# A convolution and state-space kernel: another order of the work, a convolution with stationary weights, and replicated loads in two halves on two DMA queues

## The chip, the cores and the metric

The program runs on one core of a Trainium2 chip. The core has five engines that run side by side, each with its own instruction stream: TensorE (PE in the profile; its weight loads stand apart as PEld), VectorE (DVE), ScalarE (ACT), GpSimd (POOL) and SyncE (SP). They share a memory of 128 partitions (SBUF) and a small one for sums (PSUM), and wait for each other through semaphores. Transfers between SBUF and the chip's main memory (DRAM) run on 16 DMA engines; an instruction on SP or ACT issues one, and each of the two has its own DMA queue.

The metric is device time in microseconds of one execution. The time before is the median of three runs.

## The reference

Four layers are computed on an input of shape (2, 128, 128, 128): batch, channels, rows, columns, all in float32. Layers 0 and 2 are the same function with different weights, and they hold what is changed. Cut to that:

```python
y = conv3x3(x, conv_w) + conv_b                  # 128 -> 128 channels
seq = y.reshape(B * H * W, 8, 16)                # a row of a channel: 8 tokens of 16 features
xz = einsum('nld,ed->nle', seq, in_proj_w)
xi, z = split(xz, 2)                             # 32 and 32
xc = silu(causal_conv1d(xi, conv1d_w) + conv1d_b)
dt, Bm, Cm = split(einsum('nld,ed->nle', xc, x_proj_w), [1, 17])
dt = softplus(dt * dt_proj_w + dt_proj_b)        # 8 tokens x 32
dA = exp(dt[..., None] * A)                      # 32 x 16 states, A = -exp(A_log)
dBx = dt[..., None] * Bm[:, :, None, :] * xc[..., None]
# over the 8 tokens:
h = dA[t] * h + dBx[t]
ys[t] = sum_n(h * Cm[t])
ym = (ys + D * xc) * silu(z)
out = ym @ out_proj_w.T                          # back to 16 features
# group norm over 4 groups of channels, silu, and x is added
```

Layer 1 is a gate from the density of 8 x 8 windows, and layer 3 a block of two convolutions with batch norm over the whole batch. The change does not touch these.

## The kernel before

One batch at a time goes through layer 0 (`_mamba`, `_group_norm`), layer 1 (`_density_gate`) and layer 2 (`_mamba`, `_group_norm`); layer 3 (`_basic_block`) follows for both. So `_mamba` runs four times.

In `_mamba` the image is cut into 32 tiles of four rows. One row of one channel, 128 numbers, is one sequence of 8 tokens x 16 features, so a tile has 4 x 128 = 512 sequences, and they lie along the free dimension. The state of one token, 32 inner channels x 16 states for each sequence, is 512 rows of 512 sequences, held as `NJ` = 4 blocks on 128 partitions. Within a block the partition is (n, e): 16 states n, each with `DJ` = 8 channels e.

The stages of a tile are small functions:

- `conv` (L274) runs one image row per call: for each of nine taps the 128 pixels of the row are the stationary operand and the tap's weights the moving one, 128 columns each, 36 matmuls a tile. The result has the row's columns on the partitions, so the tokens and their features, as `project` needs them. VectorE adds the bias (L293).
- `project` (L301) makes xc and z, each by two matmuls and a silu on ScalarE.
- `steps` (L315) makes dt by softplus, u = dt * xc on GpSimd (L324), and stores u into DRAM as `su` with two DMAs (L327).
- `inout` (L332) makes B and C, stores both into DRAM as `sb` (L344) and multiplies them (`prod`, L346). C of a token is stored with B of the same token.
- `own` (L348) makes the part of the output that a token gives to itself.
- `load` (L358) reads, for token t, eight rows of `su` back into all 16 groups of partitions (`ur`, 1024 KB, L363), and 16 rows of `sb` into eight partitions each (`bcr`, 512 KB, L368). These are the replicated loads. Both are issued on SP.
- `inject` (L370) multiplies `ur` and B on GpSimd into `h`.
- `token` (L375) does for each half of the blocks: two matmuls into `set` (L391), the exponential (L399), and on VectorE the product with the old state (L401), the product with C (`r`, L402) and the sum into the new state (L406). Then four matmuls sum `r` over the states into `ys` (L409). After tokens 3 and 7, VectorE adds `t1` (L420) and GpSimd multiplies by silu(z) (L421). After token 7, `finish` (L426) multiplies by the output weights, copies, takes statistics and stores.

The order is set in two steps. `put` (L445) lists each call under a step; there are `STEPS` = 7 steps a tile, one for each of the tokens 1 to 7, and a tile's earlier stages stand under negative steps, beside the tokens of the tile before. The calls are traced in that order, and the framework's scheduler then orders each engine's instructions by priority and by when it expects their inputs and buffers. Each engine executes its own stream in order. Buffers limit how far one can run ahead: three of `ur`, five of `bcr`, four of `h`, two of `r`, two of `set`, two of the common PSUM tile `one`.

Of the kernel before, what the change touches and what calls it, by code (L numbers as in the profile page):

```python
# [31 lines left out]
P = 128  # L32
NT, FT = 8, 16
DI, DS, DC = 32, 16, 4
NQ = 4
NJ = DI * DS // P
DJ = DI // NJ
NG = 4
# [11 lines left out]
def _constants(H):  # L50

    parts = {}


    neg = np.zeros((NJ, NQ, DJ, NQ, DS, DJ), np.float32)
    red = np.zeros((DS, DJ, NQ, NQ, DJ), np.float32)
    gsum = np.zeros((2, NQ, DS, 2, NJ, NQ, DJ), np.float32)
    for q in range(NQ):
        for e in range(DJ):
            neg[:, q, e, q, :, e] = -1.0  # L60
            red[:, e, q, q, e] = 1.0
        for g in range(2):
            gsum[g, q, :, g, :, q, :] = 1.0
    parts["neg"] = neg.reshape(P, -1)
    parts["red"] = red.reshape(P, -1)
    parts["gsum"] = gsum.reshape(P, -1)
    parts["group"] = np.kron(np.eye(NG), np.full((CG, CG), 1.0 / CG)).astype(np.float32)
    parts["ident"] = np.eye(P, dtype=np.float32)
    parts["neghalf"] = np.full((P, CG), -0.5, np.float32)
    for name, n in (("wy", H), ("wx", P)):  # L70
        _, frac = _bilinear(n)
        parts[name] = np.tile(frac[None, :], (P, 1))
    return _packed(parts)
# [24 lines left out]
def _mamba_layout(w):  # L98
# [24 lines left out]
    alog = np.zeros((NJ, NQ, DJ, NQ, DS, DJ), f32)  # L123
    po = np.zeros((P, NT, DI), f32)
    by_d = wx.reshape(-1, NJ, DJ)
    for q in range(NQ):
        pdt1[:, q, :, :, q, :] = by_d[0][:, :, None, None]
        pdt2[:, q, :, :, q, :] = w["dt_proj_w"][:, 0].reshape(NJ, DJ)[None, None, :, :]
        pb[:, q, :, q, :] = by_d[1 : 1 + DS].transpose(1, 2, 0)
        pc[:, q, :, q, :] = by_d[1 + DS :].transpose(1, 2, 0)  # L130
        for e in range(DJ):
            alog[:, q, e, q, :, e] = w["A_log"].reshape(NJ, DJ, DS)[:, e, :]
    for t in range(NT):
# [10 lines left out]
            "conv_b": np.tile(w["conv_b"][None, :], (P, 1)),  # L144
# [104 lines left out]
STEPS = NT - 1  # L249
AT_CONV, AT_XC, AT_DT, AT_BC, AT_G = -11, -7, -6, -6, -4  # L250
AHEAD_LOAD, AHEAD_B = 4, 2


def _mamba(tc, src, w, con, dst, scratch, stats, H):
# [14 lines left out]
    live = {}  # L269

# [3 lines left out]
    def conv(k, part):  # L274

        if part == 0:
            if k % (BAND // ROWS) == 0:
                live["band"] = _load_band(nc, bandp, src, k * ROWS, BAND, H)
            live[k] = {"py": one(), "band": live["band"]}
        xb, py = live[k]["band"], live[k]["py"]  # L280
        r = part
        for tap in range(9):
            kh, kw = divmod(tap, 3)
            nc.tensor.matmul(  # L284
                py[:, r * P : (r + 1) * P],
                lhsT=xb[:, (k * ROWS) % BAND + r + kh, kw : kw + P],
                rhs=w["conv"][:, tap, :],
                start=(tap == 0),
                stop=(tap == 8),
            )  # L290
        if part == ROWS - 1:
            y = seq.tile([P, NS], F32, tag="y", name="y")
            nc.vector.tensor_tensor(  # L293
                y.rearrange("p (r c) -> p r c", r=ROWS),
                py.rearrange("p (r c) -> p r c", r=ROWS),
                w["conv_b"].unsqueeze(1).to_broadcast([P, ROWS, P]),
                ALU.add,
            )
            live[k]["y"] = y

    def project(k):  # L301
# [3 lines left out]
        zs = s["zs"] = seq.tile([P, 2, NS], F32, tag="zs", name="zs")  # L305
# [9 lines left out]
    def steps(k):  # L315

        s = live[k]
        dt = s["dt"] = seq.tile([P, 2, NS], F32, tag="dt", name="dt")
        for g in range(2):
            pd = one()  # L320
            nc.tensor.matmul(pd, lhsT=w["dt"], rhs=s["xc"][:, g, :], start=True, stop=True)  # L321
            nc.scalar.activation(dt[:, g, :], pd, AF.Softplus, bias=w["dt_b"])  # L322
        u = s["u"] = seq.tile([P, 2, NS], F32, tag="u", name="u")
        nc.gpsimd.tensor_tensor(u, dt, s["xc"], ALU.mult)  # L324
        su = s["su"] = scratch.tile([NT, DJ, NJ, NS], F32, tag="su", name="su")
        for g in range(2):
            nc.sync.dma_start(  # L327
                out=su[g * NQ : (g + 1) * NQ].rearrange("q e j s -> j (q e) s"),
                in_=u[:, g, :],
            )  # L330

    def inout(k):  # L332

        s = live[k]
        bc = tmp.tile([P, 2, NS], F32, tag="bc", name="bc")
# [7 lines left out]
        sb = s["sb"] = scratch.tile([NT, DS, 2, NS], F32, tag="sb", name="sb")  # L343
        nc.sync.dma_start(out=sb.rearrange("t n i s -> (t n) i s"), in_=bc)  # L344
        prod = s["prod"] = tmp.tile([P, NS], F32, tag="prod", name="prod")
        nc.gpsimd.tensor_tensor(prod, bc[:, 0, :], bc[:, 1, :], ALU.mult)  # L346

    def own(k):  # L348

        s = live[k]  # L350
        t1 = s["t1"] = seq.tile([P, 2, NS], F32, tag="t1", name="t1")
        for g in range(2):
            p = one()
            nc.tensor.matmul(p, lhsT=gsum[:, g, :], rhs=s["prod"], start=True, stop=True)  # L354
            nc.scalar.copy(t1[:, g, :], p)  # L355
        nc.gpsimd.tensor_tensor(t1, t1, s["u"], ALU.mult)  # L356

    def load(k, t):  # L358

        s = live[k]  # L360
        if t < NT - 1:
            ur = s["ur", t] = st.tile([P, NJ, NS], F32, tag="ur", name="ur", bufs=3)
            nc.sync.dma_start(  # L363
                out=ur,
                in_=s["su"][t].unsqueeze(0).to_broadcast([DS, DJ, NJ, NS]),
            )
        bcr = s["bcr", t] = st.tile([P, 2, NS], F32, tag="bcr", name="bcr", bufs=5)
        nc.sync.dma_start(out=bcr, in_=s["sb"][t].unsqueeze(1).to_broadcast([DS, DJ, 2, NS]))  # L368

    def inject(k, t):  # L370
        s = live[k]
        b = s["h", t] = st.tile([P, NJ, NS], F32, tag="h", name="h", bufs=4)
        nc.gpsimd.tensor_tensor(b, s["ur", t], s["bcr", t][:, 0:1, :].to_broadcast([P, NJ, NS]), ALU.mult)  # L373

    def token(k, t):  # L375
# [3 lines left out]
        if t == 1:  # L379
            s["ys"] = [None, None]  # L380
        if t == 1 or t == NQ:
            s["ys"][g] = ps_y.tile([P, NS], F32, tag=f"ys{g}", name="ys")
            nc.tensor.matmul(s["ys"][g], lhsT=w["d"], rhs=s["xc"][:, g, :], start=True, stop=False)
        ys = s["ys"][g]
        r = st.tile([P, NJ, NS], F32, tag="r", name="r", bufs=2)
        for jp in range(2):
            pt = ps_set.tile([P, 2, NS], F32, tag="set", name="set")
            for i in range(2):
                j = 2 * jp + i
                a = j * NQ * DJ  # L390
                nc.tensor.matmul(  # L391
                    pt[:, i, :],
                    lhsT=w["rep"][a : a + NQ * DJ, q, :],
                    rhs=s["dt"][a : a + NQ * DJ, g, :],
                    start=True,
                    stop=True,
                    tile_position=(a, 0),
                )
            nc.scalar.activation(pt, pt, AF.Exp)  # L399
            js = slice(2 * jp, 2 * jp + 2)  # L400
            nc.vector.tensor_tensor(pt, pt, s["h", t - 1][:, js, :], ALU.mult)  # L401
            nc.vector.tensor_tensor(  # L402
                r[:, js, :], pt, s["bcr", t][:, 1:2, :].to_broadcast([P, 2, NS]), ALU.mult
            )
            if t < NT - 1:
                nc.vector.tensor_tensor(s["h", t][:, js, :], pt, s["h", t][:, js, :], ALU.add)  # L406
        for j in range(NJ):
            a = j * NQ * DJ
            nc.tensor.matmul(  # L409
                ys[a : a + NQ * DJ, :],  # L410
# [6 lines left out]
        if q == NQ - 1:  # L417

            v = seq.tile([P, NS], F32, tag=f"v{g}", name="v")
            nc.vector.tensor_tensor(v, ys, s["t1"][:, g, :], ALU.add)  # L420
            nc.gpsimd.tensor_tensor(v, v, s["zs"][:, g, :], ALU.mult)  # L421
            s["v", g] = v
        if t == NT - 1:
            finish(k)

    def finish(k):  # L426
        s = live.pop(k)
        po = one()
        for r in range(ROWS):
            for g in range(2):  # L430
                nc.tensor.matmul(  # L431
                    po[:, r * P : (r + 1) * P],
# [5 lines left out]
        o = seq.tile([P, NS], F32, tag="o", name="o")  # L438
        nc.scalar.copy(o, po)
        nc.vector.bn_stats(stats[:, k, :], po)  # L440
        nc.sync.dma_start(out=dst[:, k * ROWS : (k + 1) * ROWS, :].rearrange("p r w -> p (r w)"), in_=o)
# [3 lines left out]
    def put(k, at, f, *args):  # L445
        todo.setdefault(k * STEPS + at, []).append((f, (k, *args)))

    for k in range(ntile):
        for t in range(1, NT):
            put(k, t - 1, token, t)  # L450
        for part in range(ROWS):
            put(k, AT_CONV + part, conv, part)
        put(k, AT_XC, project)
        put(k, AT_DT, steps)
        put(k, AT_BC, inout)
        put(k, AT_G, own)
        for t in range(NT):
            put(k, t - AHEAD_LOAD - 1, load, t)
            if t < NT - 1:
                put(k, t - AHEAD_B - 1, inject, t)  # L460
    for at in sorted(todo):
        for f, args in todo[at]:
            f(*args)
# [309 lines left out]
```

## Time and profile before

| what | value |
|---|---|
| median of three runs | 10826.29 us (10817.6 to 10827.49) |
| profiled execution, its own time | 10815.53 us |
| its span, first to last instruction | 10813.7 us |
| granted clock of TensorE, mean | 0.897 |
| DMA moved | 1855.67 MB, mean 172 GB/s |

The page cuts the span into 40 slices of 270 us. The four runs of `_mamba` are the long stretches with DMA near 8 tenths; the gaps between are group norm and the gate, and the last 1.1 ms are layer 3. An engine's busy time does not count the time in which it waits in place or issues DMAs. A line of waits reads: who waited, for whom, the total in us, how often, the longest. A line of the chain reads: start, length, what ran.

### The profile page before, as it was taken

How to read it: one execution, taken by the hardware profiler on the slowest of the kernel's cores; microseconds unless marked ns; L12 is line 12 of the kernel's file. 1: busy time of each engine (PE TensorE's matmuls, PEld its weight loads, DVE VectorE, ACT ScalarE, POOL GpSimd, SP SyncE). 2: the span in 40 equal slices, each digit the busy share in tenths (PEclk: the TensorE clock that was granted, in tenths of full speed). 3: DMA queues.
4: the chain of work that ended last, by engine and by line, in shares of the span. 5: the costliest groups of instructions: out<-in, count | busy, mean ns of one | idle time of the engine just before them, and what ended most of it. 6: DMA issues, size and time to landing. Idle time of an engine off the chain costs nothing. (4 is left out here: it accounts for less than half of the span.)

```text
span 10813.7 us, 97333 instructions
## 1 busy us (share of the span) xinstructions
PE 8964.8 (83%) x36376; PEld 3550.2 (33%) x36376; DVE 6885.4 (64%) x6330; ACT 4590.3 (42%) x4841; POOL 5187.4 (48%) x1810
## 2 busy tenths in 40 slices
PE   7888888865888888858888888865888888859995
PEld 3333333243333333313333333253333333314442
DVE  5777777725777777756777777725777777740102
ACT  4555555422555545434555555312555555520112
POOL 5565656502666656526566566402665566620000
PEclk9999999856999999979999999756999999979997
DMA  8888888714888888868888888615888888861003
GB/s 200 202 198 198 201 199 203 176 66 116 200 203 200 196 196 203 191 193 207 199 201 201 199 200 204 170 45 133 197 202 202 199 197 199 199 182 44 22 0 118
DMA packets 510325, 1855.67 MB, mean 172 GB/s; under 512 B 42240, under 2 KB 163616, under 8 KB 395168
## 3 DMA queue, kind: packets, MB, share of 16 engines
q1 hardware_dynamic: 500640, 1815.90, 70.4%
q10 hardware_dynamic: 9216, 33.56, 0.8%
q8 instruction: 289, 4.73, 0.2%
q14 instruction: 180, 1.47, 0.1%
HBM read 1631.19 MB, written 218.10 MB: 171 GB/s over the span
## 5 line engine op out<-in xcount | busy, mean ns | idle before, releaser
L373 POOL TENSOR_TENSOR h<-ur,bcr 128x2048 f32<-128x2048 f32 x896 | 4052.8, 4526 | 2826.1 <-DMA bcr<-sb 1403.4
L399 ACT ACTIVATE set<-set 128x1024 f32<-128x1024 f32 x1792 | 1805.6, 1008 | 3009.5 <-PE set L391 2989.0
L401 DVE TENSOR_TENSOR set<-set,h 128x1024 f32<-128x1024 f32 x1792 | 2198.8, 1228 | 1007.7 <-ACT set L399 873.8
L409 PE MATMUL ys<-r,ct 128*32 128x512 f32 x7168 | 2021.5, 647 | 248.0 <-DVE r L402 247.8
L402 DVE TENSOR_TENSOR r<-set,bcr 128x1024 f32<-128x1024 f32 x1792 | 2189.0, 1222 | 48.5
L391 PE MATMUL set<-dt,rep 32*128 32x512 f32 x7168 | 2060.8, 653 | 5.0 <-DVE h L406 4.9
L406 DVE TENSOR_TENSOR h<-set,h 128x1024 f32<-128x1024 f32 x1536 | 1865.1, 1214 | 6.1 <-POOL h L373 6.1
L284 PE MATMUL one<-conv,band 128*128 128x128 f32 x9216 | 1415.1, 292 | 235.6 <-POOL band L169 215.7
L284 PEld LDWEIGHTS one<-conv,band 128*128 128x128 f32 x9216 | 1152.7, 193 | 1366.4 <-issue 1034.7
L391 PEld LDWEIGHTS set<-dt,rep 32*128 32x128 f32 x7168 | 545.0, 186 | 1077.1 <-issue 623.9
L399 ACT ACT_TABLE_LOAD x612 | 785.2, 1283 | 10.8
L354 PE MATMUL one<-prod,ct 128*128 128x512 f32 x512 | 412.9, 953 | 422.9 <-POOL prod L346 422.9
L409 PEld LDWEIGHTS ys<-r,ct 128*32 128x32 f32 x7168 | 266.8, 111 | 1300.6 <-DVE r L402 885.0
L641 DVE BATCH_NORM_STATS2 st<-pc 128x6 f32<-128x512 f32 x128 | 89.5, 699 | 904.2 <-ACT Y L640 904.2
L420 DVE TENSOR_TENSOR v<-ys,t 128x512 f32<-128x512 f32 x256 | 177.0, 691 | 759.4 <-PE ys L409 757.5
L633 PE MATMUL pc<-band,w 128*128 128x512 f32 x1152 | 496.1, 593 | 87.7 <-DVE w L625 87.7
L339 PE MATMUL one<-xc,keep 128*64 128x512 f32 x1024 | 535.3, 619 | 36.5 <-ACT dt L322 36.1
L431 PE MATMUL one<-keep,v 128*128 128x128 f32 x2048 | 348.5, 325 | 243.5 <-POOL v L421 243.5
L356 POOL TENSOR_TENSOR t<-t,u 128x1024 f32<-128x1024 f32 x128 | 299.8, 2343 | 500.1 <-ACT t L355 500.1
L633 PE MATMUL pc<-hband,w 128*128 128x512 f32 x1152 | 497.5, 595 | 6.3 <-ACT hband L675 6.3
L167 POOL MEMSET band<- 128x20 f32 x96 | 11.5, 125 | 906.2 <-PE pc L633 513.1
L640 ACT COPY Y<-pc 128x512 f32<-128x512 f32 x128 | 74.9, 585 | 874.3 <-PE pc L633 874.3
(110 smaller groups left out, 6841.8 us busy)
## 6 DMA issues: line engine op xcount, KB each, us to landing
ur<-su SPq DMA_DIRECT2D x896, 1024.0 KB
bcr<-sb SPq DMA_DIRECT2D x1024, 512.0 KB
su<-u SPq DMA_DIRECT2D x256, 256.0 KB
sb<-bc SPq DMA_DIRECT2D x128, 512.0 KB
band<-x SPq DMA_DIRECT2D x56, 640.0 KB
y<-o SPq DMA_DIRECT2D x128, 256.0 KB
g<-y SPq DMA_DIRECT2D x64, 512.0 KB
xr<-x SPq DMA_DIRECT2D x64, 512.0 KB
```

The lines of the kernel that those rows point to most:

```text
L284: nc.tensor.matmul(py[:, r * P : (r + 1) * P], lhsT=xb[:, (k * ROWS) % BAND + r + kh, kw : kw + P], rhs=w["conv"][:, tap, :], start=(tap = ...
L339: nc.tensor.matmul(p[g * NQ * DS : (g + 1) * NQ * DS, :], lhsT=w[m], rhs=s["xc"][:, g, :], start=True, stop=True)
L354: nc.tensor.matmul(p, lhsT=gsum[:, g, :], rhs=s["prod"], start=True, stop=True)
L373: nc.gpsimd.tensor_tensor(b, s["ur", t], s["bcr", t][:, 0:1, :].to_broadcast([P, NJ, NS]), ALU.mult)
L391: nc.tensor.matmul(pt[:, i, :], lhsT=w["rep"][a : a + NQ * DJ, q, :], rhs=s["dt"][a : a + NQ * DJ, g, :], start=True, stop=True, tile_posi ...
L399: nc.scalar.activation(pt, pt, AF.Exp)
L401: nc.vector.tensor_tensor(pt, pt, s["h", t - 1][:, js, :], ALU.mult)
L402: nc.vector.tensor_tensor(r[:, js, :], pt, s["bcr", t][:, 1:2, :].to_broadcast([P, 2, NS]), ALU.mult)
L406: nc.vector.tensor_tensor(s["h", t][:, js, :], pt, s["h", t][:, js, :], ALU.add)
L409: nc.tensor.matmul(ys[a : a + NQ * DJ, :], lhsT=red[:, q, :], rhs=r[:, j, :], start=False, stop=(q == NQ - 1), tile_position=(0, a),)
L431: nc.tensor.matmul(po[:, r * P : (r + 1) * P], lhsT=s["v", g][:, r * P : (r + 1) * P], rhs=w["out"][:, g, :], start=(g == 0), stop=(g == 1),)
L633: nc.tensor.matmul(pc, lhsT=w[:, tap, :], rhs=xb[:, rr + kh : rr + kh + ROWS, kw : kw + P], start=(tap == 0), stop=(tap == 8),)
```

## The change

It has six parts, all in `_mamba` and its weights.

1. The convolution is turned round: nine matmuls of 512 columns a tile with the weights stationary, spread in six calls over the slots -22 to -16, with the channels on the partitions, bias by ScalarE, and then four transposes on TensorE (`turn`) with a copy on ScalarE.
2. A step becomes two slots (`SLOTS` = 14 a tile), one for each half of a token. The sums into `ys` are a call of their own (`gather`), two slots after their half tokens; so are `gate`, `out` (in two halves), `product`, `scaled` and `own_u`.
3. The instructions of TensorE, ScalarE, VectorE and GpSimd keep the order in which they are written (`manual_schedule`); SP's queue is not in that list.
4. Partitions of the state are ordered (half of the channels, n, channel within the half) instead of (n, e). The constants and weights follow.
5. `load` is called twice for each token, once for each half of the partitions: the lower half on SP, the upper on ScalarE's queue one slot later.
6. `sb` holds C of the following token beside B, in two stores of 112 partitions, so seven loads of `bcr` serve a tile instead of eight.

```diff
+SLOTS = 2 * (NT - 1)
+CONV_AT = {-22: 1, -21: 1, -20: 2, -18: 2, -17: 1, -16: 2}
+TURN_AT, PROJECT_AT, DT_AT, U_AT, BC_AT, PROD_AT, OWN_AT, OWN_U_AT = -15, -14, -12, -10, -10, -9, (-6, -5), -4
+LOAD_AT, INJECT_AT = -9, -5
+GATHER_AT = 1
+GATE_AT = (8, 16)
+OUT_AT = (19, 20)
...
+        for tap in range(first, first + n):
             kh, kw = divmod(tap, 3)
             nc.tensor.matmul(
-                py[:, r * P : (r + 1) * P],
-                lhsT=xb[:, (k * ROWS) % BAND + r + kh, kw : kw + P],
-                rhs=w["conv"][:, tap, :],
+                py.rearrange("p (r w) -> p r w", r=ROWS),
+                lhsT=w["conv"][:, tap, :],
+                rhs=xb[:, r + kh : r + kh + ROWS, kw : kw + P],
...
+            nc.scalar.activation(yc, py, AF.Identity, bias=w["conv_b"])
+    def turn(k):
...
+        for r in range(ROWS):
+            nc.tensor.transpose(p[:, r * P : (r + 1) * P], s["yc"][:, r * P : (r + 1) * P], con["ident"])
+        s["y"] = tmp.tile([P, NS], F32, tag="y", name="y")
+        nc.scalar.copy(s["y"], p)
...
+        sb = s["sb"] = scratch.tile([NT - 1, DS, 2, NS], F32, tag="sb", name="sb")
+        nc.sync.dma_start(out=sb[:, :, 0].rearrange("t n s -> (t n) s"), in_=bc[: P - DS, 0, :])
+        nc.sync.dma_start(out=sb[:, :, 1].rearrange("t n s -> (t n) s"), in_=bc[DS:, 1, :])
...
+    def load(k, t, half):
+        s = live[k]
+        if half == 0:
+            s["ur", t] = st.tile([P, NJ * NS], F32, tag="ur", name="ur", bufs=3)
+            s["bc", t] = st.tile([P, 2, NS], F32, tag="bcr", name="bcr", bufs=5)
+        dma = (nc.sync, nc.scalar)[half].dma_start
+        ps = slice(half * P // 2, (half + 1) * P // 2)
+        es = slice(half * DH, (half + 1) * DH)
+        u = s["su"][t, es].rearrange("e j s -> e (j s)")
+        dma(out=s["ur", t][ps], in_=u.unsqueeze(0).to_broadcast([DS, DH, NJ * NS]))
+        m = s["sb"][t].rearrange("n i s -> n (i s)")
+        dma(
+            out=s["bc", t][ps].rearrange("p i s -> p (i s)"),
+            in_=m.unsqueeze(1).to_broadcast([DS, DH, 2 * NS]),
+        )
...
+            for jp in range(2):
+                put(k, 2 * (t - 1) + jp, token, t, jp)
+            put(k, GATHER_AT + 2 * t, gather, t)
...
+        for t in range(NT - 1):
+            for half in range(2):
+                put(k, LOAD_AT + 2 * t + half, load, t, half)
+            put(k, INJECT_AT + 2 * t, inject, t)
+    E = mybir.EngineType
+    with tc.manual_schedule(engines={E.PE, E.Activation, E.DVE, E.Pool}):
+        for at in sorted(todo):
+            for f, args in sorted(todo[at], key=lambda x: (x[0] is not token, x[0] is inject)):
+                f(*args)
```

## The prediction

> **What bounds the kernel now.** I read the page first, for shares, then the windows between the first and the last output of each of the four layers, to get one stage with one pattern.
>
> ```profile
> PE 8964.8 (83%) x36376; PEld 3550.2 (33%) x36376; DVE 6885.4 (64%) x6330; ACT 4590.3 (42%) x4841; POOL 5187.4 (48%) x1810
> ...
> DMA  8888888714888888868888888615888888861003
> 136.50:2170.80 2034.30, 1772.35 (x6882) 642.14 (x6878) 1542.72 (x1362) 1015.93 (x1056) 1212.08 (x379) 0.95 0.84 196
> 2711.60:4757.70 2046.10, 1780.46 (x6880) 647.56 (x6878) 1542.50 (x1362) 1015.93 (x1056) 1212.17 (x379) 0.94 0.84 195
> 4970.20:7010.60 2040.40, 1788.24 (x6882) 644.69 (x6878) 1543.34 (x1362) 1015.93 (x1056) 1211.84 (x379) 0.94 0.83 195
> 7554.20:9594.80 2040.60, 1779.45 (x6882) 645.97 (x6878) 1538.71 (x1359) 1015.30 (x1055) 1212.73 (x387) 0.94 0.84 196
> 1042.00:1060.00 18.00, 13.17 (x48) 4.95 (x44) 11.83 (x11) 9.37 (x10) 13.75 (x4) 0.91 1.02 229
> ```
>
> The columns of a window are its length, busy time of PE, PEld, DVE, ACT and POOL, granted clock, DMA share and GB/s. Each layer holds 32 tiles, so 31 periods lie in a window: 8161.4 us / 124 = 65.8 us a tile. In it PE is busy 7120.5/124 = 57.4 us, DVE 6167.3/124 = 49.7, ACT 32.8, POOL 39.1, and DMA has a share of 0.84. Nothing is full, yet several are near it. The last line shows DMA at its limit: at a share of 1.02 it moves 229 GB/s (other full stretches gave 226 to 236). So its work, 0.84 x 65.8 = 55 us, comes in bursts with about 10 us of gap in each tile. Next, who makes the others wait:
>
> ```profile
> ACT set L399 <- PE set L391: 2989.0, 1171, 9.4
> POOL h L373 <- DMA bcr<-sb: 1403.4, 323, 11.7
> ...
> DVE set L401 <- ACT set L399: 873.8, 747, 5.8
> DVE v L420 <- PE ys L409: 757.5, 134, 7.0
> ...
> DVE stats L440 <- ACT o L439: 356.7, 128, 8.2
> ```
>
> VectorE idles for the exponential (873.8), at the end of each half of the tokens for the last sums (757.5, some 5.9 us each tile) and for the output copy (356.7). The chain of waits shows why the exponentials are late in the middle of a tile: ScalarE changes its table for each activation.
>
> ```profile
> 8064.04 0.69 ACT xc L309
> 8064.74 1.28 ACT L399
> 8066.04 0.33 ACT set L399
> 8066.37 0.70 issue
> 8067.06 1.28 ACT L309
> 8068.36 0.69 ACT xc L309
> ```
>
> A 1.28 us table load stands before and after each 0.69 us activation. The page's groups have 612 + 248 + 247 + 120 = 1227 such loads under L399, L322, L309 and L313, 9.6 a tile. Before this piece the chain stays on PE from 8033.6 to 8062.7 (convolution between set and ys), and behind it it runs through POOL's 4.5 us inject. The bound is thus the order of the work within a tile, on top of a DMA load that would by itself allow about 55 us.
>
> **The change, part by part.** *DMA bytes.* Per tile now: ur 7 x 1024 KB, bcr 8 x 512, su 512, sb 512, y 256, half a band 320, together 12,864 KB (13.17 MB, which over 65.8 us gives 200 GB/s, as the page's slices have). After: C is stored one token back, so the eighth bcr load goes (-512) and sb shrinks to 448: 12,288 KB, 12.58 MB. At 229 to 231 GB/s that is 54.7 us.
>
> *PE.* 36 convolution matmuls of 128 columns cost 1415.1/128 = 11.1 us a tile (L284). Nine of 512 columns, as in L633 (496.1 + 497.5 us for 1152, 0.86 us each), cost 7.8, and four transposes as at L520 (62.9/256 = 0.25) 1.0. PE falls from 57.4 to about 55.1 us. These busy times overlap waits a little, so this is an upper figure for what PE must have.
>
> *VectorE.* L293 (0.69) moves to ScalarE. Left: 14 x (1.228 + 1.222) + 12 x 1.214 + 2 x 0.691 + 0.699 = 51.0 us. The 757.5 us wait goes, because gate now stands after the following half token (slots 8 and 16, gathers at 7 and 15); output and statistics move to slots 19 and 20, where the copy has the slot to itself. What stalls next follows from ScalarE's hand order.
>
> *ScalarE.* Four silu stand together in slot 0, two softplus in slot 2: four table loads a tile, not 9.6, saving 5.6 x 1.28 = 7.2 us. Added are yc (0.69, as L309) and y (0.58, as L342), and 14 DMA issues. An issue on this engine took 0.34 us (L498, L692), one of a replicated load on SP 0.52 (L368); I take 0.52, as the descriptors are alike: 7.3 us. ScalarE so stays near 33 + 1 us of 65, but the place matters. In slot 0, from the end of one exponential to the end of the next: 2 issues 1.04, load 1.28, silu 2 x 0.69 + 2 x 0.60, load 1.28, exponential 1.01, together 7.2 us against 3.66 us of VectorE work for one half token. Having a lead of about 1 us (set 1.06 + exponential 1.01 after the half token before last has freed its PSUM, against 3.66), it leaves VectorE idle about 2.5 to 3.5 us. Slot 2: 1.04 + 1.28 + 1.38 + 1.28 + 1.01 = 6.0, against 3.66 + 0.69 and a lead of 1.5: nothing to speak of. The compute chain is then 51 + 3.5, some 55 us.
>
> *The two queues.* Behind a load on ScalarE's queue stand the next exponential, and VectorE and PE behind that. The load waits for r of the half token before (bcr has five buffers), which ends about when this slot's exponential does; for inject three tokens back, placed three slots (about 12 us) earlier; and, for token 0, for su to have landed, two slots after u. The cover is the two slots of earlier tokens' loads in flight; if DMA is late, ScalarE pays. On SP, su, the two sb stores, band and y stand among half the loads, as now.
>
> *The gap.* Today the first ur load is issued 1014.95 - 1008.80 = 6.2 us after su, and SP passes nothing meanwhile. Afterwards ScalarE's half of token 6 is issued one slot later than SP's and may fill this. Bounds for the gap: 0 (filled) and 10.5 us (the unused 0.16 of 65.8, as now). I take 4.5, nearer the first: the stores alone need 960 KB / 230 = 4.3 us and do run.
>
> *Price of a half.* No row shows 64 partitions loaded from two queues. Upper end of the rate: 344 GB/s (the last stage moved 275 GB/s at a share of 0.80, two queues, other addresses). Lower end: half of 230, if the halves take turns with half the machinery. I take 230: the packets (8 and 4 KB), their source and their number stay. POOL's 39 us and everything outside the layers stay; six more half-token slots of filling in each layer, of 0 to 4 us, I cost at nothing, since the windows leave filling out, and keep up to 4 x 6 x 4 = 96 us for the range.
>
> *The sum.* Three resources want about 55 us. DMA with its gap ends last: 54.7 + 4.5 = 59.2 us. Saved: 124 x (65.8 - 59.2) = 820 us. The profiled execution had 10815.5 (10813.7 span and 1.8 around it), so 9995; the median of the runs shown lies 10.8 above it: 10005.
>
> [...]
>
> **The rivals.** *A. The second queue quickens the loads, and compute is the bound.* For: the last stage's 344 GB/s at full share. Against: there one queue read and the other wrote. At 55 us: 124 x 10.8 = 1340, about 9490.
>
> *B. The halves move slower than whole tiles, and the chain waits for DMA: slower.* Place: POOL's wait for bcr, 1403.4 us today. It decides where loads and rest fill the present period: 65.8 - 6.8 = 59.0 us for 11.01 MB, 187 GB/s. Against: every full stretch is above that. For: each half touches half of the partitions, and two slots pass between issue and need. At 165 GB/s: 66.7 + 6.8 = 73.5 us, 124 x 7.7 = 955 more, 11780; at 175, 69.7 us and 11310.
>
> *C. The fixed order gives part back.* ScalarE waits in place at its load pairs: seven a tile; 0.6 us at each is 4.2 us, 63.4 us a tile, 10530. It reaches no gain at 6.6/7 = 0.94 us. For: three engines near 55 us leave little slack to an engine that may not pass anything. Against: each wait counted above ends when its neighbours would wait anyway.
>
> *D. It doesn't do what it says.* The words speak of the same convolution and order, the diff changes both; if stalls and gains cancelled, 10826.
>
> **How the numbers follow.** Main case 0.45 (9800 to 10250), A 0.16, B 0.18, C 0.17, D 0.04. 0.2% (22 us) is about what a measurement of this kernel can tell from no change. Faster: main, A, and nearly all of C, 0.77; same 0.04; slower: B and a little of C, 0.19. Range: from A's compute chain, 9450, to 10800, which takes in C and the rule's price and leaves B out.
>
> **What would show it.** The windows: 59 us a tile with a DMA share above 0.9, DVE about 0.86 busy. DVE's wait for ys gone; table loads about 520 instead of 1227; DVE's wait for the exponential 3 us a tile, in slot 0. DMA at full share near 230 GB/s; below 187 is B, well above 250 with DVE over 0.9 is A. DMA-issue waits on ScalarE of a microsecond each are C. The prediction is wrong if full-share DMA moves, or if exponentials wait for something other than their set matmuls.

## The result, and the profile after

The changed kernel takes 11413.63 us (median of 4 runs, 11404.31 to 11423.97) against 10821.94 us for the kernel before on the same chip (4 runs): a ratio of 1.0548, 95% interval 1.053 to 1.0566. It is slower by 592 us, outside the forecast range of 9450 to 10800. All line numbers from here on are those of the kernel named.

First the page of the changed kernel (span 11405.3 us): busy time of the engines, then the granted clock and DMA share in 40 slices, and one window of 1600 us inside the first layer with the columns of before.

```profile
PE 8223.5 (72%) x29976; PEld 2851.6 (25%) x29976; DVE 6784.8 (59%) x6202; ACT 3785.2 (33%) x4377; POOL 5182.0 (45%) x1810
...
PEclk8888888756888888878888888856878888879997
DMA  7777777713777777776777777713777777771103
...
300.00:1900.00 1600.00, 1175.00 (x4009) 362.97 (x4001) 1105.13 (x970) 601.51 (x694) 898.33 (x283) 0.83 0.73 177
```

Every engine has less to do than before, and every engine and DMA is also busy for a smaller share. Nothing has become a bound; more time passes in which several stand at once. The starts of VectorE's first product in successive tiles lie 71.1 us apart on average (66.3 before by the same measure, 65.8 counted from output to output as in the prediction; 59.2 forecast). The mean granted clock fell from 0.897 to 0.812. The waits, as engine, operation and line, who was waited for, total us, times, longest:

```profile
ACT set L421 <- PE set L413: 3158.1, 1263, 21.0
...
DVE set L423 <- ACT set L421: 2855.3, 753, 59.0
...
POOL h L397 <- DMA bcr<-sb: 901.1, 275, 15.9
...
PE one L291 <- DMA band<-x: 623.7, 32, 72.9
PE one L291 <- DMA band<-in_x_dram: 569.7, 32, 83.1
...
ACT set L421 <- DMA ur<-su: 385.7, 34, 20.0
ACT set L421 <- DMA sb<-bc: 327.7, 32, 11.6
```

VectorE's wait for the exponential more than tripled (873.8 before). Its roots are two kinds of wait that before had no weight. TensorE waits 64 times, once in every second tile, for a convolution band to land: 1193.4 us. Four of these waits stand at the start of a layer and stay when the band is loaded early (240.8 us there); the other 60 take 952.6 us, 15.9 us each. ScalarE's exponential waits 66 times for DMAs, 713.4 us, 10.8 us each, though it reads nothing that they bring. What waits is the load that ScalarE issues ahead of it, for token 0, whose `su` and `sb` have yet to land. By the semaphore events of the trace this load stands in nearly every tile, on average 5.8 us until `su` has landed (126 of 128 tiles) and then 3.4 us until `sb` has (127); where TensorE's wait for the band lies over it, the lines above name that instead. Both happen at the same place. Token 0's upper half is loaded at slot -8 of its tile and the first convolution call stands at slot -22; with 14 slots to a tile both are slot 6 of the stream. Before VectorE's first product of slot 7 there are 11.6 us of idle time in a mean tile, before that of slot 1, behind the four silu and the load of token 4 in slot 0, there are 7.1, and all 14 slots together have 21.6.

Here is one such place in the timeline: start, length, engine, line and operation, and in brackets idle time before it and who ended it. A q behind an engine marks its queue of DMA issues.

```profile
1025.07 1.17 SPq L340 DMA_DIRECT2D su<-u  x2
...
1026.33 0.57 SPq L389 DMA_DIRECT2D bcr<-sb  x1
...
1031.25 0.55 SPq L387 DMA_DIRECT2D ur<-su  x1
...
1031.89 0.53 SPq L355 DMA_DIRECT2D sb<-bc  x1
...
1038.01 0.52 ACTq L389 DMA_DIRECT2D bcr<-sb  x1
...
1038.63 1.01 ACT L421 ACTIVATE set<-set 128x1024 f32<-128x1024 f32 x1 [10.82 <-DMA sb<-bc]
...
1039.67 1.23 DVE L423 TENSOR_TENSOR set<-set,h 128x1024 f32<-128x1024 f32 x1 [7.15 <-ACT set L421]
...
1043.44 2.07 PE L413 MATMUL set<-dt,rep 32*128 32x512 f32 x4 [7.47 <-DVE h L428]
...
1051.32 1.13 PE L413 MATMUL set<-dt,rep 32*128 32x512 f32 x4
```

`sb` is stored by SP, and in its queue the store of L355, issued at 1031.89, stood behind a load (L387, the lower half of token 0) that went only at 1031.25, when `su` had landed. The copies that it stores were done at 1021.9. The stored data landed at 1038, and until then ScalarE stood at its own load with a ready exponential behind it, and VectorE and TensorE behind that. SP's queue shows where its stores and loads are held:

```profile
SPq L387 <- POOL h L397: 3393.8, 628, 12.9
SPq L340 <- POOL u L337: 1676.8, 128, 26.6
...
SPq L387 <- DMA su<-u: 536.5, 128, 5.8
```

The last is the wait ahead of the store, once in each tile. The first, for GpSimd's inject, was 1098.6 us before (L363 there). In the kernel before, SP issued the store of `sb` ahead of token 0's load, in all 128 tiles:

```profile
1008.80 1.16 SPq L327 DMA_DIRECT2D su<-u  x2
1010.06 0.46 SPq L344 DMA_DIRECT2D sb<-bc  x1
1014.95 1.74 SPq L363 DMA_DIRECT2D ur<-su  x2
```

SP's order is the scheduler's in both kernels; in the changed one the stores stand behind that load in 120 of 128 tiles. In every second tile the band stands behind them, too:

```profile
1099.00 0.41 SPq L173 DMA_DIRECT2D band<-in_x_dram  x1
...
1103.92 0.52 ACTq L389 DMA_DIRECT2D bcr<-sb  x1
...
1108.95 2.04 PE L291 MATMUL one<-band,conv 128*128 128x512 f32 x2 [14.11 <-DMA band<-in_x_dram]
...
1110.93 2.08 PE L413 MATMUL set<-dt,rep 32*128 32x512 f32 x4
...
1113.05 1.01 ACT L421 ACTIVATE set<-set 128x1024 f32<-128x1024 f32 x1 [17.53 <-PE set L413]
1114.09 1.23 DVE L423 TENSOR_TENSOR set<-set,h 128x1024 f32<-128x1024 f32 x1 [15.94 <-ACT set L421]
```

In the hand order the band is asked for in the same call as its first matmul. TensorE meets that matmul in slot 6, stands 14 us until 10 us after the issue, and the matmuls of the next state, which need no band, stand behind it. In this tile, too, ScalarE stood at its load of token 0, until 1103.92, but TensorE stood longer. After both stalls the same four set matmuls take 2.07 or 2.08 us instead of 1.13, which they take at 1051.32. The windows of the first stall show a lower granted clock with it (the number ahead of the last two):

```profile
1036.00:1042.00 6.00, 0.00 (x0) 0.00 (x0) 2.29 (x2) 2.43 (x3) 3.81 (x1) 0.92 1.04 268
1042.00:1048.00 6.00, 4.56 (x10) 1.24 (x14) 5.97 (x7) 1.01 (x1) 0.43 (x1) 0.50 1.03 266
...
1060.00:1066.00 6.00, 5.55 (x25) 1.89 (x24) 5.11 (x5) 3.12 (x4) 3.28 (x2) 1.00 1.03 226
```

TensorE had stood from 1036.0 to 1043.4; the stretch in which it came back has a granted clock of 0.50, the one from 1060 has 1.00.

### The profile page after: what moved, and what is told of

The parts are those of the page before. It is cut to its first block, busy times and chain, and to the rows that moved or that the text cites. A ratio compares the mean times of both kernels' runs of the same rounds, so it can differ in the third digit from the quotient of the medians.

```text
span 11405.3 us, 89801 instructions
## 1 busy us (share of the span) xinstructions
PE 8223.5 (72%) x29976; PEld 2851.6 (25%) x29976; DVE 6784.8 (59%) x6202; ACT 3785.2 (33%) x4377; POOL 5182.0 (45%) x1810
## 4 chain that ended last, share of the span: by engine, by line
PE 27%; DMA 26%; DVE 18%; POOL 11%; issue 8%; ACT 7%; SPq 1%; ACTq 1%; POOLq 0%; DVEq 0%
PE pc L682 9%; POOL h L397 8%; DMA ur<-su 7%; DMA su<-u 7%; DVE set L423 6%; DVE r L424 5%; PE set L413 5%; DVE h L428 5%; PE one L322 3%; ACT set L421 3%; PE one L291 3%; DMA band<-in_x_dram 3%; DMA band<-x 3%; POOL u L337 3%; PE ys L440 2%
## 5 line engine op out<-in xcount | busy, mean ns | idle before, releaser
L421 ACT ACTIVATE set<-set 128x1024 f32<-128x1024 f32 x1792 | 1800.9, 1008 | 3945.3 <-PE set L413 3158.1
L413 PE MATMUL set<-dt,rep 32*128 32x512 f32 x7168 | 2295.3, 720 | 992.3 <-DVE h L428 991.9
L291 PE MATMUL one<-band,conv 128*128 128x512 f32 x2304 | 1293.4, 675 | 1193.4 <-DMA band<-x 623.7
L454 POOL TENSOR_TENSOR v<-v,zs 128x512 f32<-128x512 f32 x256 | 325.7, 1272 | 2910.3 <-DVE v L453 2898.6
L440 PE MATMUL ys<-r,ct 128*32 128x512 f32 x7168 | 1152.7, 718 | 2.2 <-DVE r L424 2.2
L291 PEld LDWEIGHTS one<-band,conv 128*128 128x128 f32 x2304 | 424.4, 207 | 1926.5 <-issue 1923.3
L322 PE MATMUL one<-y,keep 128*128 128x512 f32 x512 | 397.1, 920 | 473.2 <-ACT xc L319 473.1
L436 PE MATMUL ys<-xc,keep 128*128 128x512 f32 x512 | 364.3, 800 | 0.0
L337 POOL TENSOR_TENSOR u<-dt,xc 128x1024 f32<-128x1024 f32 x128 | 303.3, 2369 | 103.3 <-ACT dt L331 103.3
L440 PEld LDWEIGHTS ys<-r,ct 128*32 128x32 f32 x7168 | 152.8, 116 | 757.7 <-issue 737.3
L586 PE MATMUL pg<-xq,ct 64*32 64x256 f32 x512 | 270.9, 631 | 98.4 <-ACT xq L573 98.4
```

What stands on the lines that cost most here:

```text
L291: nc.tensor.matmul(py.rearrange("p (r w) -> p r w", r=ROWS), lhsT=w["conv"][:, tap, :], rhs=xb[:, r + kh : r + kh + ROWS, kw : kw + P], st ...
L322: nc.tensor.matmul(pz, lhsT=w["z"][:, g, :], rhs=s["y"], start=True, stop=True)
L337: nc.gpsimd.tensor_tensor(u, s["dt"], s["xc"], ALU.mult)
L413: nc.tensor.matmul(pt[:, i, :], lhsT=w["rep"][a : a + NQ * DJ, q, :], rhs=s["dt"][a : a + NQ * DJ, g, :], start=True, stop=True, tile_posi ...
L436: nc.tensor.matmul(s["ys", g], lhsT=w["d"], rhs=s["xc"][:, g, :], start=True, stop=False)
L440: nc.tensor.matmul(s["ys", g][a : a + NQ * DJ, :], lhsT=red[:, q, :], rhs=r[:, j, :], start=False, stop=(q == NQ - 1), tile_position=(0, a),)
```

## The experiments

All runs below compute the whole of the function. Two theories stood at the start: the waits in place of the fixed order (ScalarE at its loads, TensorE at the band), and the rival that halves on two queues are slow or disturb each other. Ratios are to the kernel before on the chip of the run; on the three chips used it took 10801, 10816 and 10839 us, so some tens of microseconds between runs of different chips say nothing.

**Both halves on SP.** This takes the loads off ScalarE and keeps the order of the four compute engines.

```diff
-        dma = (nc.sync, nc.scalar)[half].dma_start
+        dma = nc.sync.dma_start
```

> Both halves of every replicated load are issued on SP; nothing else differs from the changed kernel. My theory: the changed kernel loses its time where an engine that may not pass anything waits in place, in slots 6 and 7 of a tile: ScalarE at its load of token 0 (713 us of waits for su and sb, before some 66 exponentials) and TensorE at a band that has not landed (1193 us). Here ScalarE's part goes and the band's stays, so 10800 to 11100. Rival (the halves themselves move slowly, as my case B had it): the halves are still there, so within 100 us of 11414.

Measured: 10786.66 us, ratio 0.9982 (0.9971 to 0.9993). So 627 us come back. SP's own order changed with it: the stores of `sb` now stand ahead of token 0's load in all 128 tiles, and what that is worth by itself was not tested. ScalarE's waits for `su` and `sb` are gone; those of TensorE for the band have grown, as these waits show:

```profile
PE one L291 <- DMA band<-x: 887.9, 32, 72.7
...
PE one L291 <- DMA band<-in_x_dram: 847.5, 32, 84.7
```

Tiles without a band wait now have a median period of 52.8 us and those with one 79.9; the 55 us in an expectation below is the median of both kinds together, which no kind of tile takes. VectorE's idle time ahead of slot 7 has not shrunk (11.8 us after 11.6), since the band's wait fills it; that ahead of slot 1 has, from 7.1 to 3.3. So part of the gain lies at a load other than token 0's. The same halves, one behind the other on one queue, move a median of 223 GB/s in the six-microsecond stretches of the first layer at a DMA share of 0.98 or more, against 231 on two queues: the second queue adds little.

**The band earlier.** The band load becomes a call of its own, one tile (14 slots) ahead of the first matmul.

```diff
-            if at not in bands:
-                bands[at] = _load_band(nc, bandp, src, at * BAND, BAND, H)
+    def fetch(k):
+        at = k * ROWS // BAND
+        bands[at] = _load_band(nc, bandp, src, at * BAND, BAND, H)
...
+        if k % (BAND // ROWS) == 0:
+            put(k, -36, fetch)
```

> The band is loaded 14 slots before its first matmul instead of just ahead of it. Theory: TensorE's 1193 us of waits for the band go, but in those tiles ScalarE's wait for token 0 (about 11 us) was hidden beneath and comes out, so half of it is gained: 10800 to 11050, with ScalarE's waits for su and sb about twice 713 us. Rival (halves move slowly): the band's wait moves to inject, no gain above 150 us.

Measured: 10776.56 us, 0.9977 (0.9962 to 0.9991), a gain of 637 us, and ScalarE's waits for `su` and `sb` grew from 713.4 to 1174.5 us; there are 122 of them now, one in nearly every tile:

```profile
ACT set L422 <- DMA sb<-bc: 630.3, 60, 12.0
...
ACT set L422 <- DMA ur<-su: 544.2, 62, 11.6
```

The two stalls lay over each other: ScalarE's load of token 0 stood as long in the changed kernel, in tiles with a band wait and without (9.2 and 9.3 us), and shows now that TensorE no longer stands longer.

**The stores of B and C from ScalarE's queue.** If only SP's queue delays `sb`, its stores can go from the engine that made the data.

```diff
-        nc.sync.dma_start(out=sb[:, :, 0].rearrange("t n s -> (t n) s"), in_=bc[: P - DS, 0, :])
-        nc.sync.dma_start(out=sb[:, :, 1].rearrange("t n s -> (t n) s"), in_=bc[DS:, 1, :])
+        nc.scalar.dma_start(out=sb[:, :, 0].rearrange("t n s -> (t n) s"), in_=bc[: P - DS, 0, :])
+        nc.scalar.dma_start(out=sb[:, :, 1].rearrange("t n s -> (t n) s"), in_=bc[DS:, 1, :])
```

> The two stores of sb are issued on ScalarE's queue, right behind the copies that make their source, instead of on SP behind a load that waits for inject. Theory: sb lands some 6 us earlier, ScalarE's waits for sb (328 us) go and those for su stay, and the band's stay: 11050 to 11300. Rival (queue order doesn't matter, DMA is simply full): within 100 us of 11414.

Measured: 11452.94 us, 1.06 (1.058 to 1.0621): a miss, nothing came back. `sb` is in time, but `ur` of the same token still waits for `su`, which SP stores as before, and behind it the load of B and C stands once more, in 122 tiles and for 385 us, until an earlier half of `ur` on SP has landed, which is what this line names:

```profile
ACT set L421 <- DMA ur<-su: 655.2, 65, 12.2
```

The place is the load itself, not one of its sources. Why a load waits for another load is told under "Token 0 alone on SP".

**Halves and partition order in the kernel before.** Only parts 4 and 5 of the change, in the kernel before, whose order comes from the scheduler.

```diff
-            nc.sync.dma_start(
-                out=ur,
...
+        for half in range(2):
+            dma = (nc.sync, nc.scalar)[half].dma_start
+            ps = slice(half * P // 2, (half + 1) * P // 2)
...
```

> The kernel before with only what the words name: the new partition order of the state, and each replicated load in two halves, the lower on SP, the upper on ScalarE's queue. Order by the scheduler, old convolution, eight loads of bcr. Theory (halves cost little; the loss is in the hand order): 10700 to 11000. Rival (halves or the second queue cost): 11200 or more. If the second queue helps: below 10600.

Measured: 12723.42 us, 1.1776 (1.1753 to 1.18). Far off, and the opposite of harmless; we come back to it below.

**Both cures together.** The edits of the first two experiments.

```diff
-        dma = (nc.sync, nc.scalar)[half].dma_start
+        dma = nc.sync.dma_start
...
+        if k % (BAND // ROWS) == 0:
+            put(k, -36, fetch)
```

> Both causes taken away at once: all halves on SP, the band 14 slots early. Theory: nothing waits in place in slots 6 and 7 any more, and every tile takes the 55 us that the median tile of the all-on-SP run took, unless DMA binds: halves sent one after the other on SP moved 209 to 221 GB/s at full share there, so 12.58 MB take about 58 us. 9450 to 9900. Rival (the two waits cover others, a third takes their place): 10200 or more, little better than either alone.

Measured: 9812.67 us, 0.9072 (0.9058 to 0.9085), as the theory had it. The window of the first layer:

```profile
300.00:1900.00 1600.00, 1358.02 (x4851) 426.70 (x4851) 1351.99 (x1189) 737.82 (x837) 1100.83 (x343) 0.90 0.95 217
```

The period is 58.25 us, VectorE idles 2.7 us a tile before its products, and DMA has a share of 0.95. Each cure alone brought some 630 us; together they bring 1601. That is more than the 592 us that the change lost. But this run takes all seven pairs of loads from ScalarE's queue, not token 0's alone; "Token 0 alone on SP" parts the two.

**Whole loads.** Also with the partition order of before and one load of 128 partitions on SP for each token.

```diff
-        if half == 0:
...
-        dma(out=s["ur", t][ps], in_=u.unsqueeze(0).to_broadcast([DS, DH, NJ * NS]))
+        u = s["su"][t].rearrange("e j s -> e (j s)")
+        nc.sync.dma_start(out=s["ur", t], in_=u.unsqueeze(0).to_broadcast([DS, DJ, NJ * NS]))
...
```

> As the last, but with the old partition order and each load as one of 128 partitions on SP. If halves on one queue move slower than whole tiles (216 against 230 GB/s at full share) and DMA binds, this is faster than the last by up to 58 - 55 = 3 us a tile, 380 us: 9350 to 9600. If halves cost nothing: within 60 us of the last.

Measured: 9694.89 us, 0.8965 (0.8951 to 0.8978), the fastest version of all. Its window:

```profile
300.00:1900.00 1600.00, 1344.51 (x4912) 420.18 (x4908) 1368.00 (x1215) 742.07 (x844) 1105.27 (x345) 0.92 0.91 217
```

It moves the same 217 GB/s at a share of 0.91 instead of 0.95, thus 238 GB/s at full share against 228. In a fixed order, halves, which also mean 33.5 DMAs a tile instead of 19.5, cost 118 us, 1.2%.

**Token 0 alone on SP.** The band early, and only the pair at which ScalarE waited taken from its queue.

```diff
-        dma = (nc.sync, nc.scalar)[half].dma_start
+        dma = (nc.sync, nc.scalar if t else nc.sync)[half].dma_start
```

> Two queues as in the changed kernel, band early, but both halves of token 0 on SP, so that ScalarE never stands before su and sb. Theory (ScalarE's loss is the wait for token 0's data alone): 9450 to 9900, like all on SP. Rival (each load on ScalarE waits in place for inject or r, case C of the prediction): 10200 to 10700.

Measured: 10620.21 us, 0.9823 (0.9807 to 0.984), within what rival C allowed and 808 us behind the same kernel with all loads on SP. So of the 1601 us the two waits named above are worth 793, and the other pairs on ScalarE's queue 808. The waits move to those later pairs:

```profile
ACT set L422 <- DMA bcr<-sb: 539.1, 60, 10.3
...
ACT yc L301 <- DMA ur<-su: 282.9, 47, 8.9
...
ACT set L422 <- DMA ur<-su: 247.1, 42, 7.5
```

VectorE's idle time is 14.8 us a tile, spread over slots 1 (5.8), 9 (3.6) and 13 (3.2). The lines name the landing of replicated loads, which no load of this run reads. The trace's semaphore events tell why: all DMAs of the program use eight completion semaphores, 574 or 575 issues on each here and in the changed kernel, 350 or 351 in the one before, and an issue stands until the DMA ahead of it on its own semaphore has landed: of the 4590 issues with one ahead in the changed kernel's trace, and of the 2798 in that of the kernel before, none went earlier. At 596 of ScalarE's loads, and for 1892 us in all, the last event before the issue is such a landing, mostly of a half of `ur` issued on SP; for the load at 1028.12, for instance, the half issued at 1019.03 landed at 1028.04. The end of an inject on GpSimd, which frees a buffer of `ur`, comes last for 45 us, VectorE's work for 277. Part of this time ScalarE had nothing else to do. The changed kernel has the same wait: 412 us at the loads of tokens 3 and 4, the second of which stands in slot 0.

**Halves in the kernel before, all on SP.** Was ScalarE's queue to blame for the 18%?

```diff
-            dma = (nc.sync, nc.scalar)[half].dma_start
+            dma = nc.sync.dma_start
```

> The kernel before with the new partition order and every load in two halves, both on SP. Against the split over two queues (12723) it tells the halves from the queue. If ScalarE's queue is the whole loss: 10800 to 11000 (halves at 216 instead of 230 GB/s make a full DMA stretch of 57 us some 3 us longer, part of it hidden). If the halves are: 12000 or more.

Measured: 12786.55 us, 1.1822 (1.1799 to 1.1846): no. Here GpSimd stands in place, in three waits that before came to 90.7, 99.0 and 500.1 us:

```profile
POOL v L432 <- DVE v L431: 2690.3, 195, 25.6
POOL u L325 <- ACT dt L323: 1342.0, 115, 28.6
POOL t L357 <- ACT t L356: 828.1, 119, 9.2
```

**Whole loads on two queues.** The fastest version, with the loads of tokens 1, 3 and 5 on ScalarE, one slot later. It has fewer DMAs than the halves, so it tells the number of DMAs from the place of the issue.

```diff
-        nc.sync.dma_start(out=s["ur", t],
+        dma = (nc.sync, nc.scalar)[t % 2].dma_start
+        dma(out=s["ur", t],
...
-            put(k, LOAD_AT + 2 * t, load, t)
+            put(k, LOAD_AT + 2 * t + t % 2, load, t)
```

> Whole loads of 128 partitions, band early, but the loads of tokens 1, 3 and 5 on ScalarE's queue, one slot later; token 0 stays on SP. In the two-queue run with halves ScalarE's loads waited 1175 us for the landing of earlier DMAs: the program keeps eight DMAs under way, and halves double their number. If that is what ScalarE waits for, fewer DMAs (19.5 instead of 33.5 a tile) let it pass: 9650 to 9950. If a load on ScalarE costs by its place alone (it waits for inject or r): three pairs instead of six, about half of that run's 810 us: 10050 to 10300. If the second queue quickens the loads: below 9600.

Measured: 10191.51 us, 0.9402 (0.938 to 0.9424), 497 us slower than with all of them on SP, as the theory of place alone had it. The wait, and one instance from the timelines of ScalarE and GpSimd:

```profile
ACT yc L301 <- issue: 1061.8, 120, 18.1
```

```profile
1040.18 1.01 ACT L419 ACTIVATE set<-set 128x1024 f32<-128x1024 f32 x1 [2.52 <-PE set L411]
...
1045.57 4.49 POOL L395 TENSOR_TENSOR h<-ur,bcr 128x2048 f32<-128x2048 f32 x1 [10.11 <-DMA bcr<-sb]
...
1050.09 0.52 ACTq L385 DMA_DIRECT2D ur<-su  x1
1050.71 0.56 ACTq L387 DMA_DIRECT2D bcr<-sb  x1
1051.37 0.69 ACT L301 ACTIVATE yc<-one,keep 128x512 f32<-128x512 f32 x1 [10.18 <-issue]
```

Between the end of the exponential (1041.2) and the load (1050.09) ScalarE does nothing for 8.9 us. The load goes 0.03 us after GpSimd's inject has ended, which frees its buffer. It is so at 126 loads of `ur` in this run, for 926 us; waits for an earlier DMA on the load's own semaphore make 15. So the two-queue runs lose at the same place for different reasons: with halves mostly for a completion semaphore, with whole loads mostly for inject. No pair is halved here, and the second queue still costs.

**The kernel before with twice as many loads.** Its loads cut in two along the free dimension, 128 partitions each, all on SP.

```diff
+            for i in range(0, NJ, 2):
+                nc.sync.dma_start(
+                    out=ur[:, i : i + 2, :],
...
```

> The kernel before, with every replicated load cut in two along the free dimension (two blocks each, B and C apart), all on SP, 128 partitions, old partition order, old number of bytes. The halves by partitions cost 1970 us under the scheduler's order on one queue, and the other queue changed nothing. If the number of DMAs is the cause (eight under way, and another order from the scheduler): 12300 to 13000. If the 64 partitions or the new partition order are: within 200 us of 10816.

Measured: 10698.77 us, 0.9876 (0.986 to 0.9892): twice the replicated loads do no harm there, they even gain 1.2%. So the 18% of the two runs with partition halves aren't the number of DMAs, nor the queue. They have another order of instructions: in the run just told, all 4841 of ScalarE's instructions stand in the order of the kernel before, and TensorE's differ from it at 40 of 36376 places; in the run with partition halves on SP, ScalarE has 4533 instructions and TensorE's differ at 18912 places. That the scheduler's other order is the whole of the 18% was not shown by itself, since no run gave the halves the order of before.

**SP unburdened the other way.** The fastest version with the stores of `sb` (the edit shown above) and of `y` on ScalarE's queue.

```diff
-            nc.sync.dma_start(out=dst[:, k * ROWS : (k + 1) * ROWS, :].rearrange("p r w -> p (r w)"), in_=o)
+            nc.scalar.dma_start(out=dst[:, k * ROWS : (k + 1) * ROWS, :].rearrange("p r w -> p (r w)"), in_=o)
```

> The fastest so far (whole loads on SP, band early), with the stores of sb and y on ScalarE's queue behind the copies that make them, so that SP's queue holds loads, su and band alone. SP waited 92 us at sb and 479 us at bcr for sb; DMA has a share of 0.91. If SP's queue still holds loads back: 9500 to 9650. If DMA and VectorE (51 of 57 us) are the limit: within 60 us of 9695.

Measured: 9899.61 us, 0.9138 (0.9121 to 0.9155), 205 us slower than the fastest version: a miss again. Stores issued behind their own producer also cost on this queue, and why was not taken apart; the period is 59.0 us against 57.3.

## Why the prediction was wrong, point by point

**The step that failed.** "On SP, su, the two sb stores, band and y stand among half the loads, as now." It was not as now. Before, the scheduler had placed the issue of the band a median of 171 us ahead of its first matmul; the hand order writes it into the same call, 10 us ahead. I costed no lead for the band at all, though the diff shows the load and the matmul side by side. It cost TensorE 952.6 us of waits (7.4 us a tile), and moving this load alone brought 637 us. Nor did the stores of `sb` stand as before: the prediction reads that "SP passes nothing meanwhile" between `su` and the first load of `ur`, but the store of `sb` went out there, at 1010.06, and afterwards it stood behind that load.

**The second step.** "The cover is the two slots of earlier tokens' loads in flight; if DMA is late, ScalarE pays." For token 0 there is no such cover: its data must first be stored, and the store of `sb` stands on SP behind a load that waits for `su` to land. I named the wait (su landed, "two slots after u") and then priced only the issue, 0.52 us. The wait was 9.2 us in a mean tile. For the other tokens the cover failed where an issue stood for its completion semaphore, a wait that the prediction doesn't have.

**Rival C** was the right mechanism with the wrong place and size. I had 0.6 us at each of seven pairs, and a turn into a loss at 0.94 us. Measured: most of it at one pair, where the lines of waits alone give 713.4/128 = 5.6 us a tile, already near the 6.6 us that the whole gain was worth; with the band on top, the gain was overdrawn. With that pair taken away, the later ones cost 808 us, 6.3 us a tile. And I argued against C that "each wait counted above ends when its neighbours would wait anyway"; the timeline shows the reverse, an engine that stands with ready work behind it.

**The clock** was a term I didn't have. All 152 stalls of TensorE of over 5 us in the changed kernel's trace, and all 15 in that of the kernel before, are followed by a granted clock of 0.50. How much of the 592 us this makes was not taken apart.

**The terms that held.** Table loads: forecast about 520, counted 507 under L421, L331 and L319. VectorE's wait for `ys`, 757.5 us before, is 2.8 us. The compute chain: forecast some 55 us, measured 52.8 in tiles without a band wait, in which VectorE is busy for 48.7 us and not 51; its stall behind the four silu: 2.5 to 3.5, measured 3.3, both with all loads on SP. The gap and the bytes: forecast 54.7 + 4.5 = 59.2 us; with both waits cured 58.25, which is 12.58 MB at 228 GB/s, 55.2 us, and 3 us of gap. Whatever lies outside the tile periods I had at no cost, and it stayed: counted between VectorE's first products, 2586 us before and 2583 after. So the arithmetic of the work was right, and the waits of the order were missing from it.

**A and B.** A is refuted: at a full DMA share halves on two queues move a median of 231 GB/s, as whole loads did before, and two versions were faster without the second queue, by 808 and 497 us. B is refuted as a cause: they run at 208 GB/s or more in every full six-microsecond stretch of the changed kernel's first layer, above the 187 at which B would decide (its 6.8 us were my estimate for the 1.57 MB that a tile moves besides the 11.01 MB of its loads, at 230 GB/s). The range also takes in "the rule's price", a price for halves that no run shows. What the runs showed of halves in the hand order: 58.25 us a tile with all of them on one queue, and 118 us in all, 1.2%, above whole loads.

## What to carry to other kernels

When a scheduler's order is replaced by one written by hand, give each load and each store its own lead, and look at what stands ahead of it in its queue: here TensorE stood 15.9 us on average at 60 bands, and work that needed no band stood behind it. In the changed kernel a load on ScalarE's queue, 0.52 us to issue, was a wait of 9.2 us in a mean tile; put a DMA into a compute engine's order only where its data and buffer are ready by then. When two waits lie at one place, cure both before judging either: here each alone gave 630 us and both 1601. When more DMAs are issued, look at what each issue waits for besides its data and its buffer: here it was an earlier landing, for 1892 us in one run.

## What the runs showed of the hardware that was not expected

In the trace of the changed kernel the granted TensorE clock falls to 0.50 in a stall and stays there after work has come back. In the first stretch shown it fell at 1041.1, 5.1 us after TensorE's last matmul, and rose at 1051.3, 7.9 us after work had come back at 1043.4. At the band wait it had been at 0.50 since 1088.8, twenty microseconds before the band's matmul; from 1085 to 1087 TensorE had been busy for only 0.28 and 0.25 of each microsecond. It rose at 1116.2, 7.2 us after work had come back at 1108.95. In the whole trace TensorE stands for more than 5 us 152 times, from the end of one matmul to the start of the next, and each time the clock is 0.50 1.5 us after work comes back; it rises a median of 6.9 us after work comes back, 3.7 at the least. What makes it fall and rise was not shown.

The program's DMAs use eight completion semaphores, and in the traces of both kernels no issue went before the DMA ahead of it on its semaphore had landed (4590 issues in the changed kernel, 2798 in the one before): ScalarE stood 1892 us for that in one run with halves.

The rate at a full DMA share isn't one number: in six-microsecond stretches of the first layer at a share of 0.98 or more the median is 231 before and in the changed kernel, 223 with halves on one queue and 240 with whole loads in the hand order, and single stretches reach from 196 to 313, among them the two shown with 266 and 268, in which TensorE stood or came back.
